# Four array quarters and two PSUM banks for a depthwise convolution, and a last pass with six banks, in a four-layer state-space network

## The chip, the cores and the metric

The kernel runs on one core of a Trainium2 chip. The metric is the device time of one launch in microseconds (us). A core has five engines that each work through their own instructions in order: TensorE (PE in the profile, with its weight loads as PEld), VectorE (DVE), ScalarE (ACT), GpSimd (POOL) and SyncE (SP), which here issues every DMA. Engines wait for one another by semaphores.

## The reference

Four layers run over four images of 64 x 64 pixels with 96 channels. Each layer is a token mixer and a feed-forward block, both with a residual sum and a normalisation ahead. The mixer of layer 0 is a gated linear recurrence over the 4096 pixels. Layers 1 to 3 are selective scans, with 192 inner channels, 16 states and four orders in which the pixels are visited:

```python
xz = ln(x) @ in_proj.T ; u, z = split(xz)        # 192 channels each
u = silu(conv3x3_depthwise(u) + conv_b)          # each channel with its own 9 taps
for each of 4 orders:                            # rows, columns, and both reversed
    delta, B, C = projections(u)
    h[t] = exp(delta[t] * A) * h[t-1] + delta[t] * u[t] * B[t]
    y[t] = C[t] . h[t] + D * u[t]
x = x + (ln(y1 + y2 + y3 + y4) * silu(z)) @ out_proj.T
x = x + feed_forward(ln(x))                      # operands rounded to an 8-bit float
```

The change touches the depthwise convolution of `u`, and the last mixer end and feed-forward block of the last image. What is computed stays the same.

## The kernel before, in words

**Three parts in a row.** `gated` (lines 1050 to 1283) does layer 0 of all images. `scans` (860 to 1047) does twelve stages, one for each pair of layer 1 to 3 and image. Line 1303 then finishes the last image alone: it joins the four orders, normalises, gates, projects out, and runs the feed-forward block.

**A stage of scans.** A stage has 24 items: two directions, four segments of 1024 pixels, three chunks of 128 rows. An item has 16 steps, one for each state, so the twelve stages have 4608 steps. In a step DVE multiplies a row block in PSUM (`bc`) by `du`, and then runs the scan that makes `h`. `bc` comes from PE (`b_rows`, line 904), from two buffers of two banks each; `b_rows(k + 1)` is issued in step `k` and can overwrite its buffer only after the scan of step `k - 1`. ACT makes `da`, POOL multiplies `h` by `c`, and PE adds the products up in `acc` (`add_quarters`, line 940). `add_quarters` uses the array as four tiles of 64 x 64, with 512 columns each, and the two row halves of the array write two different banks.

**What runs beside the steps.** While stage `s` scans, a `Job` (708 to 738) does the rest of the work between the stages for the next one, as Python generators whose `yield`s cut it into rounds. `between` (616 to 706) makes them: first `joins`, `mixers` and `feeds` (the end of the layer before), then `takes` (normalisation and `in_proj`) and `convolves`. Each of these handles 8 strips of 512 pixels. `Job.step` is called once in each step of the scan, and adds `rate` to a credit; each whole credit is one round, in which every chain of the job advances to its next `yield`. So the rate, 1.65 rounds a step, sets where in a stage the job's instructions stand. In the instruction stream of PE they stand after `b_rows(k + 1)` and ahead of `accumulate(k - 3)`. Two other chains advance once a step ahead of the job: `chain` (`prepare_chunk`, the next item's `dt_proj` and `delta`) and `segment` (`next_segment`, the next segment's `x_proj`). At step 0 of each third chunk line 1004 drains `segment` at once, as far as its second `x_proj_b`; at step 13 lines 1022 to 1024 drain both. In stage step 22.4 (item 22, step 4) the job has to be done.

**Banks.** PSUM has eight banks here: four for `bc`, two for `acc`, and two (`tag="ps"`, lines 123 to 132) that all of the above share. `banks["free"]` is a count kept at build time. A chain that has yielded `True` does not advance while no bank is free; one that has yielded a function waits until it returns true. A released bank counts as free from the end of the step (`settle`).

**The convolution.** `convolve` (564 to 614) computes one strip. The first 128 channels are nine matmuls with a diagonal 128 x 128 matrix of taps (`tap_lo`) over 512 pixels, all into one bank, one round each; an ACT copy takes the bank to SBUF. The last 64 channels stand twice on the partitions, and take six matmuls (`tap_hi`).

**Normalisations.** `Norm.measure` puts a variance on the list `pending`. `logarithms` (240) takes the logarithm of all pending ones on ACT, and only then `Norm.settle` can exponentiate and refine on POOL. In `Job.step`, logarithms are taken when no chain could advance for `patience` rounds, and elsewhere by the scan's own code. In line 1303 the patience is 1 and the rate 1.4.

Of the kernel before, what the change touches and what calls it, by code (L numbers as in the profile page):

```python
# [10 lines left out]
F32 = mybir.dt.float32  # L11
# [7 lines left out]
HW = 64  # L19
# [6 lines left out]
T = 1024  # L26
MM = 512
G = MM // 128
NSTRIP = L // MM
SR = MM // HW  # L30
# [69 lines left out]
def metaformer(ctx: ExitStack, tc: tile.TileContext, x, l0_ab, l0_rest, ssm, ffn, out):  # L100
# [8 lines left out]
    pbc = ctx.enter_context(tc.tile_pool(name="pbc", bufs=2, space=bass.MemoryType.PSUM))  # L109

    def sb(bufs, tag, shape, dtype=F32):
        return pools[bufs].tile(shape, dtype, tag=tag, name=tag)

    def const(name, shape, dtype=F32):
        return pools[1].tile(shape, dtype, name=name)

    def wide():
        return pbc.tile([128, T], F32, tag="bc", name="bc")


    banks = {"free": 2, "back": 0}

    def bank(name):
        banks["free"] -= 1
        return pbc.tile([128, MM], F32, tag="ps", name=name)

    def release():
        banks["back"] += 1

    def settle():  # L130
        banks["free"] += banks["back"]
        banks["back"] = 0
# [107 lines left out]
    def logarithms():  # L240
        for n in pending:
            act.activation(n.r, n.v, AF.Ln)
            n.known = True
        pending.clear()
# [319 lines left out]
    def convolve(im, layer, s, hold):  # L564

        lo, hi = hold["pads"].pop(s)
        taps = weights[layer]
        w = taps.w
        raw = []
        groups = (  # L570
            [(taps.lo[:, t, :], lo[:, t // 3 : t // 3 + SR, t % 3 : t % 3 + HW]) for t in range(9)],
            [(taps.hi[:, t, :], hi[:, 0:SR, t : t + HW]) for t in range(3)]
            + [(taps.hi[0:64, 3 + t, :], hi[0:64, 2 : 2 + SR, t : t + HW]) for t in range(3)],
        )
        for i, group in enumerate(groups):
            ps = bank("conv")
            for at, (lhs, rhs) in enumerate(group):
                pe.matmul(ps, lhs, rhs, start=at == 0, stop=at == len(group) - 1)
                yield
            v = sb(1, f"u{i}", [128, MM])  # L580
            act.copy(v, ps)
            release()
            yield i == 0
            raw.append(v)
        for i, v in enumerate(raw):
            act.activation(v, v, AF.Silu, bias=w[:, W_CB + i : W_CB + i + 1])
        gate_z(im, s + 1, hold)
        yield
        yield
        t = slice(s * MM, (s + 1) * MM)  # L590
        cols_a, part_c = hold["cols"]
        sp.dma_start(out=im.u[0, 0:64, t], in_=raw[0][0:64])
        sp.dma_start(out=im.u[1, 0:64, t], in_=raw[0][64:128])
        sp.dma_start(out=im.u[2, 0:64, t], in_=raw[1][0:64])
        for p, src, dst, c0, nc_ in (
            (slice(0, 128), raw[0], cols_a, 0, HW),
            (slice(0, 64), raw[1], part_c, 0, HW // 2),
            (slice(64, 128), raw[1], part_c, HW // 2, HW // 2),
        ):
            pool.tensor_copy(  # L600
                dst[p].rearrange("p (c r) -> p r c", r=HW)[:, SR * s : SR * s + SR, :],
                src[p].rearrange("p (r c) -> p r c", c=HW)[:, :, c0 : c0 + nc_],
            )
            if p.start or p.stop == 128:
                yield
        if s == NSTRIP - 1:
            yield
            sp.dma_start(out=im.u[1, 64:128, :], in_=cols_a[0:64])
            sp.dma_start(out=im.u[0, 64:128, :], in_=cols_a[64:128])
            for k in range(2):  # L610
                sp.dma_start(
                    out=im.u[2, 64:128, k * L // 2 : (k + 1) * L // 2],
                    in_=part_c[64 * k : 64 * k + 64],
                )

    def between(im, layer, dst=None):


        hold = {"in": {}, "pads": {}, "z": {}}
        new = dram.tile([L, C], F32, tag="x", name="x") if dst is None else dst  # L620

        def columns():
            return sb(1, "cols_a", [128, L]), sb(1, "part_c", [128, L // 2])

        def first():
            if layer:
                cols_a, part_c = hold["cols"] = columns()
                sp.dma_start(out=cols_a[0:64], in_=im.y[1, 64:128, :])
                sp.dma_start(out=cols_a[64:128], in_=im.y[0, 64:128, :])
                for k in range(2):  # L630
                    sp.dma_start(
                        out=part_c[64 * k : 64 * k + 64],
                        in_=im.y[2, 64:128, k * L // 2 : (k + 1) * L // 2],
                    )
                load_y(im, 0, hold)
            yield
            yield
            yield

        yield [Chain(first())]  # L640
        done = {"y": 0, "x": 0, "end": 0}

        def joins():
            for s in range(NSTRIP):
                yield lambda: done["x"] > s - 2
                yield True
                yield from join_orders(im, s, hold)
                done["y"] += 1

        def mixers():  # L650
            for s in range(NSTRIP):
                yield lambda: done["end"] > s - 2 and (
                    layer == 0 or (done["y"] > s and hold["y", s][1].known)
                )
                if layer:
                    yield from mixer_out(im, layer, s, hold)
                else:
                    yield from measure_x(im, s, hold)
                done["x"] += 1

        def feeds():
            for s in range(NSTRIP):
                yield lambda: done["x"] > s and hold["x", s][1].known
                yield from feed_forward(im, layer, s, hold, new)
                done["end"] += 1

        yield [Chain(f()) for f in (feeds, mixers, joins)[: 3 if layer else 2]]
        if dst is not None:
            return

        def second():
            if layer + 1 not in weights:
                weights[layer + 1] = Weights(layer + 1)
                for _ in range(4):
                    yield
                weights[layer + 1].derive()
                for t in range(0, 15, 3):
                    yield
                    weights[layer + 1].derive_taps(range(t, t + 3))
            im.x = new  # L680
            im.u = dram.tile([3, 128, L], F32, tag="u", name="u")
            im.z = dram.tile([DI, L], F32, tag="z", name="z")
            hold["cols"] = columns()
            hold["in"][0] = load_x(im, 0)
            yield
            yield

        yield [Chain(second())]
        done = {"in": 0, "out": 0}

        def takes():
            for s in range(NSTRIP):
                yield lambda: done["out"] > s - 3
                yield from take_in(im, layer + 1, s, hold)
                done["in"] += 1

        def convolves():
            yield lambda: done["in"] > 0
            gate_z(im, 0, hold)
            for s in range(NSTRIP):  # L700
                yield lambda: done["in"] > min(s + 1, NSTRIP - 1)
                yield True
                yield from convolve(im, layer + 1, s, hold)
                done["out"] += 1

        yield [Chain(f()) for f in (convolves, takes)]

    class Job:
# [23 lines left out]
                    logarithms()  # L732
                    self.waited = 0

        def finish(self):
            while not self.done:
                self.step()
                settle()


# [545 lines left out]
    for i, im in enumerate(images):  # L1286
        im.src = x[i * L : (i + 1) * L, :]
        im.dst = out[i * L : (i + 1) * L, :]
    with tc.tile_pool(name="pl0", bufs=1, space=bass.MemoryType.PSUM) as pl0:
        gated(images, Job(between(images[0], 0), 2.6, patience=1), pl0)  # L1290
    stages = [(im, layer) for layer in range(1, 4) for im in images]
    jobs = []
    for at in range(len(stages)):
        jobs.append([])
        if at + 1 < len(stages):
            im, layer = stages[at + 1]
            jobs[-1].append(Job(between(im, layer - 1), 1.65))

        for im in {10: images[:2], 11: images[2:3]}.get(at, ()):
            jobs[-1].append(Job(between(im, 3, im.dst), 2.6))  # L1300
    with tc.tile_pool(name="pac", bufs=1, space=bass.MemoryType.PSUM) as pac:
        scans(stages, jobs, pac)
    Job(between(images[-1], 3, images[-1].dst), patience=1).finish()

# [115 lines left out]
```

## Time and profile before

| what | us |
|---|---|
| median of 3 runs (lowest, highest) | 19681.59 (19680.81, 19689.28) |
| the profiled execution, its own time | 19688.32 |
| its span, first to last instruction | 19686.5 |
| layer 0, up to the first scan of 1024 | 1817.2 |
| twelve stages of scans, first to last scan's start | 17574.1 |
| from the last scan's start to the end | 295.2 |

The profile comes from one execution. A group's line gives engine, operation, output and inputs, count, then busy time in us and the mean duration of one in ns, and after the last bar the idle time of the engine just ahead of it with what ended it. All lines stand on L78, because one helper issues every operation, so groups are told apart by their tiles: `bc` and `h` are the two DVE operations of a step, `conv` the convolution, `acc` the sum, `y_t` the joins, `x_proj_b` and `x_proj_c` the segment's projections. An fp32 matmul stands as two records. PEclk is the share of TensorE's full clock that was granted.

### The profile page before, as it was taken

What the parts mean: (1) busy time and instruction counts of PE and PEld (TensorE: products, weight loads), DVE (VectorE), ACT (ScalarE), POOL (GpSimd) and SP (SyncE); (2) the same over time, 40 slices, a digit from 0 to 9 for tenths busy, and PEclk for the clock granted to TensorE, in tenths of its full rate; (3) what the DMA queues carried; (4) which work ended last, traced back from release to release, by engine and by line L of the source; (5) the groups of instructions that cost most, each with busy time, mean ns of one, the idle gap of its engine ahead of it and who ended that gap; (6) DMA issues with size and microseconds to landing.
All of it is one profiled execution on the core that took longest, in us unless ns stands there. A gap on an engine that the chain in (4) does not pass through costs nothing. (4 is left out here: it accounts for less than half of the span.)

```text
span 19686.5 us, 224801 instructions
## 1 busy us (share of the span) xinstructions
PE 16267.7 (83%) x70400; PEld 4750.9 (24%) x70400; DVE 17666.9 (90%) x13768; ACT 12256.8 (62%) x19331; POOL 15495.8 (79%) x10086
## 2 busy tenths in 40 slices
PE   8998787787888887787887888787888888888876
PEld 3332121121122222222222222222222222222223
DVE  6757999999999999999999999999999999998884
ACT  4544665665665665665666666666666666666664
POOL 3435888888888888888888888888888888878884
PEclk9998787787887797797797787797887787787886
DMA  2213676666676667666666676666666666676663
GB/s 52 50 48 87 169 185 168 170 187 164 171 189 173 166 184 182 168 185 178 170 188 176 170 186 172 170 188 174 171 186 172 170 189 174 171 187 169 165 176 89
DMA packets 1269876, 3192.65 MB, mean 162 GB/s; under 512 B 440336, under 2 KB 440560, under 8 KB 1262544
## 3 DMA queue, kind: packets, MB, share of 16 engines
q1 hardware_dynamic: 1268688, 3178.27, 61.5%
q8 instruction: 568, 9.31, 0.2%
q14 instruction: 620, 5.08, 0.1%
HBM read 2818.81 MB, written 308.28 MB: 159 GB/s over the span
## 5 line engine op out<-in xcount | busy, mean ns | idle before, releaser
L78 POOL TENSOR_TENSOR c<-h,c 128x1024 f32<-128x1024 f32 (+1 forms) x4992 | 11334.8, 2277 | 3377.8 <-DVE h L78 1478.0
L78 DVE TENSOR_TENSOR_SCAN h<-da,carry,bc 128x1024 f32<-128x1024 f32 x4608 | 10795.4, 2343 | 530.3 <-POOL c L78 17.0
L78 PE MATMUL acc<-c,twice 64*64 64x512 f32 x36864 | 6215.7, 751 | 20.1 <-POOL c L78 20.0
L78 ACT ACTIVATE da<-delta,decay 128x1024 f32<-128x1024 f32 x4608 | 5280.9, 1147 | 1491.5 <-DVE h L78 1475.6
L78 DVE TENSOR_TENSOR bc<-du,bc 128x1024 f32<-128x1024 f32 x4608 | 5565.6, 1208 | 488.4 <-PE bc L78 461.6
L78 PE MATMUL bc<-bs,sel 96*128 96x512 bf16 x9216 | 3384.4, 455 | 2343.3 <-DVE h L78 2235.9
L78 ACT COPY carry<-h 128x1 f32<-128x1 f32 x3456 | 649.5, 188 | 3374.5 <-DVE h L78 3368.7
L78 PEld LDWEIGHTS <-sel 96*128 96x128 bf16 x9216 | 552.2, 101 | 7301.0 <-DVE h L78 5519.2
L78 PEld LDWEIGHTS acc<-c,twice 64*64 64x64 f32 x36864 | 1130.7, 153 | 2799.4 <-issue 1860.2
L78 ACT ACT_TABLE_LOAD x1155 | 1481.9, 1283 | 36.5 <-DVE mv L78 20.3
L78 PE MATMUL conv<-pad,tap_lo 128*128 128x512 f32 x1728 | 906.5, 634 | 0.0
L78 PE MATMUL dt_proj<-rows,w 12*128 12x512 f32 x1152 | 826.5, 804 | 6.4 <-ACT delta L78 6.4
L78 ACT ACTIVATE du<-e,ones 128x1024 f32<-128x1024 f32 x576 | 659.3, 1145 | 199.3 <-POOL delta L78 194.5
L78 POOL TENSOR_TENSOR delta<-delta,du 128x1024 f32<-128x1024 f32 x288 | 679.8, 2361 | 72.0 <-ACT du L78 70.3
L78 PE MATMUL x_proj_b<-u,xp 128*108 128x512 f32 x1152 | 687.6, 713 | 46.4 <-DMA xp<-in_ssm 15.5
L78 PE MATMUL x_proj_c<-u,xp 128*32 128x512 f32 x1152 | 642.0, 672 | 76.1 <-ACT rows L78 67.0
L78 POOL TENSOR_TENSOR e<-e,du 128x1024 f32<-128x1024 f32 x288 | 679.8, 2360 | 2.4 <-ACT du L78 2.4
L78 ACT ACTIVATE c<-c,l_bias 128x512 f32<-128x512 f32 x384 | 263.6, 686 | 670.5 <-PE c L78 665.9
L78 POOL TENSOR_TENSOR du<-delta,u 128x1024 f32<-128x1024 f32 x288 | 680.4, 2363 | 0.1
L78 POOL TENSOR_TENSOR delta<-delta,e 128x1024 f32<-128x1024 f32 x288 | 678.8, 2357 | 0.1
L78 PE MATMUL conv<-pad,tap_hi 128*128 128x512 f32 (+1 forms) x1152 | 601.8, 624 | 0.6 <-ACT u L78 0.5
L78 DVE TENSOR_TENSOR_SCAN h<-da,l_carry,bc 128x512 f32<-128x512 f32 x384 | 491.4, 1280 | 41.9 <-DVE bc L78 2.3
(152 smaller groups left out, 15200.8 us busy)
## 6 DMA issues: line engine op xcount, KB each, us to landing
c<-cs SPq DMA_DIRECT2D x9216, 256.0 KB, 4.2
u<-u SPq DMA_DIRECT2D x288, 512.0 KB, 6.7
y<-y SPq DMA_DIRECT2D x1152, 128.0 KB, 3.2
y<-y SPq DMA_DIRECT2D x144, 512.0 KB, 6.8
xr<-x SPq DMA_DIRECT2D x224, 192.0 KB, 5.1
u<-u SPq DMA_DIRECT2D x288, 128.0 KB, 3.6
pad<-y SPq DMA_DIRECT2D x288, 128.0 KB, 4.9
z<-zl SPq DMA_DIRECT2D x96, 256.0 KB, 2.0
```

What stands on the lines that cost most here:

```text
L78: ins = f(*a, **k).ins
```

## The change

- Nine matmuls of 128 x 128 by 512 columns become nine times four of 64 x 64 by 256 columns: only the diagonal quarters of the taps, for each half of the channels and each half of the strip's eight rows. The two halves of the channels write two banks.
- One ACT copy of 128 x 512 becomes four of 64 x 256.
- `convolves` starts a strip only when both shared banks are free. The second part takes a bank after that, as before.
- `bc` moves to a PSUM pool of its own, closed after the last stage; a pool of six banks then serves the last image.
- The rate of the job between stages rises from 1.65 to 1.75.
- The last image runs at a rate of 3, with six banks, and takes logarithms after each step in which any are pending.

```diff
+        raw = [sb(1, f"u{i}", [128, MM]) for i in range(2)]
+        two = [bank("conv_a"), bank("conv_b")]
+        half = SR // 2
+        for t in range(9):
+            for k in range(2):
+                p = slice(64 * k, 64 * k + 64)
+                for j in range(2):
+                    o, y = 64 * (j ^ k), t // 3 + half * j
+                    pe.matmul(
+                        two[k][o : o + 64, 0 : MM // 2],
+                        taps.lo[p, t, p],
+                        lo[p, y : y + half, t % 3 : t % 3 + HW],
+                        start=t == 0,
+                        stop=t == 8,
+                        tile_position=(64 * k, o),
+                    )
+            yield
+        for k in range(2):
+            p = slice(64 * k, 64 * k + 64)
+            for j in range(2):
+                o = 64 * (j ^ k)
+                act.copy(raw[0][p, j * MM // 2 : (j + 1) * MM // 2], two[k][o : o + 64, 0 : MM // 2])
             release()
...
-                yield True
+                yield lambda: banks["free"] > 1
                 yield from convolve(im, layer + 1, s, hold)
...
-        def finish(self):
+        def finish(self, eager=False):
             while not self.done:
                 self.step()
+                if eager and pending:
+                    logarithms()
                 settle()
...
-            jobs[-1].append(Job(between(im, layer - 1), 1.65))
+                jobs[-1].append(Job(between(im, layer - 1), 1.75))
...
-    Job(between(images[-1], 3, images[-1].dst), patience=1).finish()
+    with tc.tile_pool(name="pend", bufs=6, space=bass.MemoryType.PSUM) as pend:
+        banks.update(free=6, back=0, pool=pend)
+        Job(between(images[-1], 3, images[-1].dst), 3, patience=1).finish(eager=True)
```

More of the change, by code (lines that the diff above doesn't have):

```diff
@@ L115, in const @@
         return pools[1].tile(shape, dtype, name=name)
+    wides = []
     def wide():
-        return pbc.tile([128, T], F32, tag="bc", name="bc")
-    banks = {"free": 2, "back": 0}
+        return wides[0].tile([128, T], F32, tag="bc", name="bc")
+    banks = {"free": 2, "back": 0, "pool": pbc}
     def bank(name):
         banks["free"] -= 1
-        return pbc.tile([128, MM], F32, tag="ps", name=name)
+        return banks["pool"].tile([128, MM], F32, tag="ps", name=name)
     def release():
@@ L568, in convolve @@
         w = taps.w
[L569 to L581, printed above, removed]
-            release()
-            yield i == 0
-            raw.append(v)
+        raw = [sb(1, f"u{i}", [128, MM]) for i in range(2)]
[20 more added lines that the diff above has]
+                act.copy(raw[0][p, j * MM // 2 : (j + 1) * MM // 2], two[k][o : o + 64, 0 : MM // 2])
+            release()
+        yield True
+        ps = bank("conv")
+        group = [(taps.hi[:, t, :], hi[:, 0:SR, t : t + HW]) for t in range(3)]
+        group += [(taps.hi[0:64, 3 + t, :], hi[0:64, 2 : 2 + SR, t : t + HW]) for t in range(3)]
+        for at, (lhs, rhs) in enumerate(group):
+            pe.matmul(ps, lhs, rhs, start=at == 0, stop=at == len(group) - 1)
+            yield
+        act.copy(raw[1], ps)
+        release()
+        yield
         for i, v in enumerate(raw):
@@ L1288, in metaformer @@
         im.dst = out[i * L : (i + 1) * L, :]
[L1289 to L1296, printed above, removed]
-            jobs[-1].append(Job(between(im, layer - 1), 1.65))
[L1299 to L1302, printed above, removed]
-    Job(between(images[-1], 3, images[-1].dst), patience=1).finish()
+    with tc.tile_pool(name="pbig", bufs=2, space=bass.MemoryType.PSUM) as wides_pool:
+        wides.append(wides_pool)
+        with tc.tile_pool(name="pl0", bufs=1, space=bass.MemoryType.PSUM) as pl0:
+            gated(images, Job(between(images[0], 0), 2.6, patience=1), pl0)
+        stages = [(im, layer) for layer in range(1, 4) for im in images]
+        jobs = []
+        for at in range(len(stages)):
+            jobs.append([])
+            if at + 1 < len(stages):
+                im, layer = stages[at + 1]
+                jobs[-1].append(Job(between(im, layer - 1), 1.75))
+            for im in {10: images[:2], 11: images[2:3]}.get(at, ()):
+                jobs[-1].append(Job(between(im, 3, im.dst), 2.6))
+        with tc.tile_pool(name="pac", bufs=1, space=bass.MemoryType.PSUM) as pac:
+            scans(stages, jobs, pac)
+    with tc.tile_pool(name="pend", bufs=6, space=bass.MemoryType.PSUM) as pend:
+        banks.update(free=6, back=0, pool=pend)
+        Job(between(images[-1], 3, images[-1].dst), 3, patience=1).finish(eager=True)
 def _layer0(W_in, b_in, W_out, b_out, gamma, beta):
```

## The prediction, made before the changed kernel was run

> **What bounds the kernel now.** I read the page first, then DVE's waits, then busy time by stretch, and last the timeline around single waits.
>
> ```profile
> PEclk9998787787887797797797787797887787787886
> L78 DVE TENSOR_TENSOR_SCAN h<-da,carry,bc 128x1024 f32<-128x1024 f32 x4608 | 10795.4, 2343 | 530.3 <-POOL c L78 17.0
> L78 PE MATMUL acc<-c,twice 64*64 64x512 f32 x36864 | 6215.7, 751 | 20.1 <-POOL c L78 20.0
> L78 DVE TENSOR_TENSOR bc<-du,bc 128x1024 f32<-128x1024 f32 x4608 | 5565.6, 1208 | 488.4 <-PE bc L78 461.6
> L78 PE MATMUL conv<-pad,tap_lo 128*128 128x512 f32 x1728 | 906.5, 634 | 0.0
> ```
>
> The twelve stages belong to DVE: 1.208 + 2.343 = 3.551 us a step, and successive steps start 3.604 us apart where nothing disturbs them. 4608 x 3.604 = 16607 of the 17574 us. Of the other 967, DVE's own smaller work (joins, normalisations, `x_proj` remainders) is some 750. So faster matmuls can only win where PE makes DVE wait. The view of DVE's waits, over the scans:
>
> ```profile
> DVE bc L78 <- PE bc L78: 461.6, 271, 20.7
> DVE x L78 <- PE out_proj L78: 29.9, 24, 3.4
> ```
>
> 461.6 us is all there is, with 21 us of it one wait. Where it lies decides. Busy time by stretch: layer 0 while it convolves, the last image's fill and run, a convolving part of stage 4 (items 13 to 20), and the part ahead of it:
>
> ```profile
> core 0: us, PE busy (x) PEld busy (x) DVE busy (x) ACT busy (x) POOL busy (x), PEclk, DMA share, GB/s
> 940.00:1480.00 540.00, 498.82 (x1249) 196.17 (x1249) 292.50 (x384) 242.66 (x494) 181.61 (x330) 0.93 0.19 47
> ...
> 19391.00:19421.00 30.00, 3.19 (x21) 0.45 (x17) 2.56 (x2) 1.01 (x1) 3.91 (x2) 0.59 0.68 147
> 19421.00:19687.00 266.00, 174.75 (x856) 108.91 (x856) 30.22 (x144) 103.02 (x226) 64.86 (x136) 0.50 0.13 33
> 8355.00:8845.00 490.00, 435.32 (x1808) 119.94 (x1804) 459.66 (x270) 343.58 (x553) 415.99 (x256) 0.92 0.69 184
> 7568.00:8355.00 787.00, 628.02 (x3168) 196.43 (x3168) 744.03 (x627) 515.07 (x811) 668.17 (x411) 0.80 0.67 173
> ```
>
> Three different limits. Layer 0 is PE's (92% busy, DVE 54%). In the stages DVE is at 94%. The end is nobody's: PE 66%, ACT 39%, all waiting in chains. DVE's waits (us in total, times, longest) in the convolving part of stage 4:
>
> ```profile
> DVE bc L78 <- PE bc L78: 9.8, 5, 4.0
> ```
>
> and in the part ahead of it, where no convolution runs:
>
> ```profile
> DVE bc L78 <- PE bc L78: 21.9, 15, 5.0
> ```
>
> **Two rules of the Trainium skill.** "TensorEngine Tiling (Array Packing)", Theoretical Speedup, offers up to four times for operands small in both dimensions; Key Properties adds that a change of tiling mode drains the array. The trace has the same four-quarter form in `acc`: 6215.7 us / 36864 records x 8 = 1.349 us for four quarters of 512 columns, against 2 x 0.525 = 1.049 us (906.5 / 1728) for a full matmul of 512. So quarters run together, at 1.29 times the price. I go by this row: half the columns, about 0.67 us a tap.
>
> "TensorE: Matmul & The Clock Gate", What's actually happening, says that too little activity drops the array to half rate. Here the granted clock is 0.92 where the convolution runs, 0.80 ahead of it, and 0.50 all through the end although PE is 66% busy there. Taking work off PE may therefore lower its clock, and in the stages I do not turn saved PE time into time one for one; for the end I go by 0.50 again.
>
> **The change part by part.** Sums are against the profiled execution, 19688.3 us (span 19686.5, 1.8 around it); the median 19681.6 lies 6.7 lower, and the forecast takes the same difference from it.
>
> *1. The taps in layer 0.* Eight strips have 72 taps. In the layer-0 stretches the tiles of `conv` hold PE for 123.97 us in 240 records, 1.033 us a tap. Against 0.67: 0.36 x 72 = 26 us. If the extra 0.30 us of a quarter group is fixed (0.52 + 0.30 = 0.82), 15; with no overhead (0.52), 37. Both banks held at once can delay the next strip's preparation; counting rounds, it ends at step 7 to 9 of 12 instead of 7, in time for the next strip. With PE 92% busy I take **-20** (range -37 to +10).
>
> *2. The taps in the stages.* 88 strips. PE loses 88 x 9 x (1.05 - 0.67) = 300 us of work, but DVE waits only 9.8 us a stage there. One of the five waits (4.0 us) falls in a stretch of `dt_proj`, `x_proj_c` and `acc` with no convolution in it; another (3.3) partly waits for `in_xt` on ACT. I give the taps 4 us a stage: 11 x 4 = **-44** (range 0 to -108).
>
> *3. The four copies.* ACT rows: 0.582 us for 128 x 512, 0.252 for 128 x 64, hence an estimated 0.39 for 256 columns. Four are 1.57 instead of 0.58: +1 us a strip, 96 us in all on an engine that is 70% busy there. `da`, queued behind them, is issued two steps ahead, and DVE waits 7 us for it in all. **0**; uncovered, at most 1 us a strip.
>
> *4. Both banks.* I counted the order round by round, for both versions, as the code writes it. For the version before, the count puts the convolutions in items 13 to 20, as the trace does. For the new one, with 1.75, the job still ends by step 21.7, ahead of its limit at 22.4, so no stage stops for it. While the taps hold both banks (nine rounds), `chain`, `segment` and `takes` cannot take one. `segment` then runs late, and line 1004 must draw 2 to 4 of its rounds at once, ahead of `b_rows(k + 1)`: about three times a stage, never before the change. Such a draw holds three `x_proj` matmuls, 3 x 1.19 (2 x 0.596) = 3.6 us of PE. `b_rows` runs a step ahead, which covers about as much at full clock and less at a low one. I take 1 us each: 11 x 3 = **+33** (range 0 to 4 us each, +132).
>
> *5. The rate.* The joins' first matmul moves from step 4 of a stage to step 3. It waits for a DMA:
>
> ```profile
> 7589.28 0.77 PE L78 MATMUL y_t<-ident,pad 128*128 128x128 f32 x2 [5.69 <-DMA pad<-y]
> ...
> 7594.65 1.23 DVE L78 TENSOR_TENSOR bc<-du,bc 128x1024 f32<-128x1024 f32 x1 [4.96 <-PE bc L78]
> ```
>
> Behind it on PE stand `acc` and the next `b_rows`, for which DVE waits. The landing stays, the matmul stands one step earlier, so DVE stops up to 3.6 us longer, in the eight stages whose job begins with joins: 0 to +29; I take 2.5 each, **+20**. SP's loads stand where they stood, at step 0. The rest of the joins gets 6% denser and the item after the job emptier: 0.
>
> *6. The end.* Its first 30 us (last sum, store, loads) stay. Then 266 us hold 174.75 us of PE work. Before, logarithms wait until every chain stands still:
>
> ```profile
> POOL t L78 <- ACT norm L78: 127.2, 6, 49.1
> DVE st L78 <- ACT yt L78: 100.5, 16, 32.7
> ```
>
> and of ACT's groups there:
>
> ```profile
> L78 ACT ACT_TABLE_LOAD x10 | 12.8, 1283 | 0.1
> ```
>
> Ten table loads are five groups of logarithms, as the count has it; then come 16 single ones, so up to 32 loads, +28 us on ACT, which has 103 of 266 in use. In return the three chains no longer stop together, and with six banks none waits for one. From 19421 to 19600 PE was busy 136.6 of 179 us (76%); fully interleaved work reaches 92% in layer 0. At 85%: 174.75 / 0.85 = 206, plus the last strip's way through the feed-forward block, some 18 us (19653 to 19671 in the chain), is 224 instead of 266: **-42**. Ends: all of PE's time back to back, 175 + 18, -73; the added loads on the chain and nothing won, +28.
>
> Sum: -20 - 44 + 0 + 33 + 20 - 42 = **-53**: 19635 in that execution, **19629** as a median (-0.27%).
>
> **Rivals.**
> - *The end doesn't shrink* (its chain is latency, and table loads eat what eager logarithms win): -20 - 44 + 53 = -11, **19671**. For it: ACT, POOL and DVE each wait over 60 us there for one another. Against: PE idles 24% even where three strips could overlap.
> - *Slower: the draws at the third chunks.* Place: PE ahead of `b_rows` at step 0 of an item. At 4 us each (the size of the largest such wait in the part above) 132, with the joins at 29: -20 - 44 - 42 + 161 = +55, **19737**. The draws decide against the change from 86 / 33 = 2.6 us each on. For it: PE is 89% busy there and cold at times; against: a step of slack.
> - *The convolution frees all of its part:* 11 x 9.8 = -108, layer 0 -37, end -73, joins +20, draws 0: -198, **19484**. Against it: the 4 us wait without a convolution.
> - *The quarters don't run together*, four times 0.52 = 2.1 us a tap: the `acc` row excludes it.
>
> **How the numbers follow.** A measurement of this kernel tells about 0.2% (39 us) from no change. Forecast 0.54, with its own range 19600 to 19665, of which 0.46 lies below 19642; end flat 0.20; slower 0.14; all freed 0.12. Faster 0.46 + 0.12 = 0.58, same 0.08 + 0.20 = 0.28, slower 0.14. The range goes from 19550 to 19720: it leaves out about half of each outer rival.
>
> **What would show it.** `conv<-pad,tap_lo` with four times the records and 0.52 to 0.82 us of PE per tap; the 461.6 us between 430 and 480; first waits of a stage near 7.5 us; new waits of DVE at step 0 or 1 of items 14, 17 and 20; the end at 240 to 265 us from the last scan's start, at clock 0.50, with about 30 table loads. I am wrong if the wait for PE drops by 150 us, if the draws cost over 2.6 us each, or if the clock in the end rises.

## The result, and the profile after

The change makes the kernel slower: 19813.76 us (median of 4 runs, 19794.9 to 19825.05) against 19685.43 (4 runs, 19680.81 to 19696.65), a ratio of 1.0066 with a 95% interval from 1.0054 to 1.0078. The forecast was 19629. The profiled execution took 19825.05 us, its span is 19823.2. Cut at the same three points as before:

| part | before | after | difference | forecast |
|---|---|---|---|---|
| layer 0 | 1817.2 | 1754.4 | -62.8 | -20 |
| twelve stages of scans | 17574.2 | 17849.8 | +275.6 | +9 |
| from the last scan's start | 295.2 | 219.1 | -76.1 | -42 |

Both outer parts won more than forecast, and the stages lost it all. The page of after, with the lines that answer to those shown of before:

```profile
PEclk9998786786887897887887887797887887888786
L78 DVE TENSOR_TENSOR_SCAN h<-da,carry,bc 128x1024 f32<-128x1024 f32 x4608 | 10797.5, 2343 | 559.7 <-ACT da L78 34.3
L78 PE MATMUL acc<-c,twice 64*64 64x512 f32 x36864 | 6163.7, 745 | 39.7 <-POOL c L78 39.7
L78 DVE TENSOR_TENSOR bc<-du,bc 128x1024 f32<-128x1024 f32 x4608 | 5571.4, 1209 | 677.1 <-PE bc L78 651.0
```

DVE's two operations of a step last as long as before, to the nanosecond or one off. What grew stands behind the last bar: the wait for PE ahead of `bc` went from 461.6 to 651.0 us. The groups of PE, the taps now in two tiles:

```profile
L78 PE MATMUL conv_a<-pad,tap_lo 64*64 64x256 f32 x3456 | 502.2, 403 | 0.0
L78 PE MATMUL conv_b<-pad,tap_lo 64*64 64x256 f32 x3456 | 501.6, 403 | 5.6 <-ACT zh L78 5.6
```

The two tiles run side by side. Together they hold PE for 514.4 us (the records' union), 0.595 us for each of 864 taps, against 906.5 us and 1.049 before. So the change does to PE what it says. Busy time by stretch: layer 0 while it convolves, the last image's fill and run, the convolving part of stage 4, and the part ahead of it:

```profile
910.00:1440.00 530.00, 497.12 (x1758) 195.70 (x1756) 316.31 (x415) 257.26 (x547) 191.82 (x349) 0.94 0.20 49
19604.00:19640.00 36.00, 9.37 (x59) 4.76 (x56) 3.01 (x4) 1.49 (x2) 3.74 (x2) 0.58 0.77 166
19640.00:19824.00 184.00, 156.25 (x818) 105.17 (x818) 29.13 (x142) 112.17 (x233) 65.00 (x136) 0.50 0.15 40
8310.00:8840.00 530.00, 419.88 (x2240) 117.22 (x2240) 474.19 (x276) 348.46 (x567) 425.52 (x273) 0.88 0.65 174
```

In the end PE is 85% busy instead of 66%, still at clock 0.50. In the convolving part of stage 4 PE fell from 89% to 79%, its clock from 0.92 to 0.88, and DVE's share from 94% to 89%: PE has less to do, and DVE waits for it more. DVE's waits there were 9.8 us for `bc` and 2.2 for `rows`; now:

```profile
DVE bc L78 <- PE bc L78: 26.6, 15, 4.9
DVE rows L78 <- ACT bs L78: 10.0, 3, 4.3
DVE h L78 <- ACT da L78: 4.2, 4, 2.5
```

What PE itself waits for tells why. Before, over the whole run (us in total, times, longest):

```profile
PE y_t L78 <- DMA pad<-y: 116.5, 12, 23.3
PE in_xt L78 <- ACT xh L78: 64.4, 41, 5.8
PE z L78 <- ACT pad L78: 1.3, 3, 0.4
PE in_proj L78 <- ACT hq L78: 0.4, 1, 0.4
```

And after:

```profile
PE y_t L78 <- DMA pad<-y: 160.6, 12, 23.2
PE z L78 <- ACT pad L78: 97.7, 37, 7.2
PE in_proj L78 <- ACT hq L78: 58.8, 15, 5.8
PE in_xt L78 <- ACT xh L78: 17.8, 13, 4.4
```

`in_proj` and `z` belong to `takes`, and both waits are new: 1.7 us became 156.5. One of them in the timeline of stage 4 (start and duration in us, the idle time ahead of it in brackets):

```profile
8514.48 0.38 PE L78 MATMUL conv_a<-pad,tap_lo 64*64 64x256 f32 x2
...
8522.99 1.06 PE L78 MATMUL in_xt<-ident,xh 128*96 128x128 f32 x4
...
8527.56 1.12 PE L78 MATMUL dt_proj<-rows,w 12*128 12x512 f32 x2
...
8541.90 1.02 PE L78 MATMUL in_proj<-hq,w 96*128 96x512 f32 x2
...
8548.61 1.28 ACT L78 ACT_TABLE_LOAD   x1
8549.91 1.15 ACT L78 ACTIVATE du<-e,ones 128x1024 f32<-128x1024 f32 x1
...
8551.14 1.28 ACT L78 ACT_TABLE_LOAD   x1
8552.43 1.15 ACT L78 ACTIVATE da<-delta,decay 128x1024 f32<-128x1024 f32 x1
...
8553.49 1.37 ACT L78 COPY pad<-in_proj 64x512 f32<-64x512 f32 x3
...
8554.91 1.97 PE L78 MATMUL z<-hq,w 96*64 96x512 f32 x2 [7.22 <-ACT pad L78]
...
8558.73 1.04 PE L78 MATMUL bc<-bs,sel 96*128 96x512 bf16 x2
...
8559.80 1.23 DVE L78 TENSOR_TENSOR bc<-du,bc 128x1024 f32<-128x1024 f32 x1 [3.79 <-PE bc L78]
```

Read from the top: the taps end at 8514.9 and give their banks back. Then `takes` (`in_xt`) and `prepare_chunk` (`dt_proj`), which both had waited for a bank, run side by side, and what they ask of ACT queues there one behind the other. `prepare_chunk`'s `du<-e` and the table loads stand ahead of the copy that empties `in_proj`'s bank. `z` stops PE for 7.22 us until that copy is done, `bc` stands behind `z` in PE's stream, and DVE loses 3.79 us. In the step before, DVE had lost 2.46 us to `da`, which stood behind the same `du<-e` and table loads.

### The profile page after: what moved, and what is told of

It reads as the page before. It is cut to its first block, busy times and chain, and to the rows that moved or that the text cites. A ratio compares the mean times of both kernels' runs of the same rounds, so it can differ in the third digit from the quotient of the medians.

```text
span 19823.2 us, 235330 instructions
## 1 busy us (share of the span) xinstructions
PE 15940.5 (80%) x75584; PEld 4692.2 (24%) x75584; DVE 17681.6 (89%) x13768; ACT 12257.0 (62%) x19560; POOL 15494.2 (78%) x10086
## 5 line engine op out<-in xcount | busy, mean ns | idle before, releaser
L78 DVE TENSOR_TENSOR bc<-du,bc 128x1024 f32<-128x1024 f32 x4608 | 5571.4, 1209 | 677.1 <-PE bc L78 651.0
L78 PEld LDWEIGHTS acc<-c,twice 64*64 64x64 f32 x36864 | 1178.9, 153 | 2601.7 <-issue 1709.7
L78 PE MATMUL conv<-pad,tap_hi 128*128 128x512 f32 (+1 forms) x1152 | 675.8, 693 | 0.2 <-ACT u L78 0.2
L78 PE MATMUL y_t<-ident,pad 128*128 128x128 f32 (+1 forms) x1536 | 413.8, 359 | 162.6 <-DMA pad<-y 160.6
```

The costliest lines, as they stand in the source:

```text
L78: ins = f(*a, **k).ins
```

## The experiments

Fifteen kernels, each with a profile and timed beside the kernel before. The table splits the profiled executions as above; the last column compares medians with the kernel before on the same chip and in the same session, where its median was 19667.8 to 19685.4.

| kernel | layer 0 | stages | end | median | ratio (95%) |
|---|---|---|---|---|---|
| before | 1817.2 | 17574.2 | 295.2 | 19685.43 | |
| after | 1754.4 | 17849.8 | 219.1 | 19813.76 | 1.0066 (1.0054 to 1.0078) |
| a1_end_only | 1805.7 | 17583.4 | 218.7 | 19609.55 | 0.9965 (0.9953 to 0.9978) |
| a2_order_only | 1772.3 | 17799.5 | 295.1 | 19862.91 | 1.0094 (1.0080 to 1.0108) |
| a3_taps_only | 1797.5 | 17594.1 | 294.7 | 19679.56 | 0.9997 (0.9989 to 1.0006) |
| a4_rate_only | 1806.2 | 17557.4 | 295.2 | 19647.58 | 0.9987 (0.9981 to 0.9994) |
| b4_end_two_banks | 1800.2 | 17581.4 | 235.8 | 19619.49 | 0.9971 (0.9960 to 0.9982) |
| c1_order_half_taps | 1760.1 | 17813.0 | 295.5 | 19856.88 | 1.0092 (1.0078 to 1.0106) |
| c2_rate_two | 1776.4 | 17810.4 | 218.0 | 19802.28 | 1.0062 (1.0049 to 1.0075) |
| c3_start_only | 1786.9 | 17594.3 | 295.3 | 19692.94 | 1.0011 (1.0005 to 1.0018) |
| c4_best | 1761.7 | 17554.6 | 218.5 | 19545.78 | 0.9932 (0.9920 to 0.9944) |
| d1_takes_wait | 1761.4 | 17591.2 | 295.5 | 19630.92 | 0.9977 (0.9969 to 0.9984) |
| d2_scan_chains_wait | 1793.1 | 17680.4 | 295.1 | 19771.51 | 1.0047 (1.0033 to 1.0060) |
| d3_four_copies | 1766.1 | 17832.7 | 295.2 | 19879.00 | 1.0102 (1.0088 to 1.0115) |
| e1_segment_free | 1773.5 | 17601.7 | 295.4 | 19680.84 | 1.0003 (0.9995 to 1.0011) |
| e2_chunk_free | 1769.4 | 17697.2 | 295.3 | 19775.26 | 1.0058 (1.0045 to 1.0071) |
| e3_takes_spread | 1766.7 | 17744.2 | 217.5 | 19730.53 | 1.0035 (1.0022 to 1.0049) |

How far a single execution carries: layer 0 has the same code in before, a1, a4 and b4, and took 1800 to 1817 us; the stages have the same code in before, a1 and b4, and took 17574 to 17583. But 33 executions of the kernel before, timed beside the first kernels, lie between 19641 and 19703 us. So a difference of less than some 40 us between two single executions is not read unless the medians bear it out.

### The four parts, each alone

**a1_end_only** takes the changed last line and what it needs, with the old convolution and rate:

```diff
-    Job(between(images[-1], 3, images[-1].dst), patience=1).finish()
+    with tc.tile_pool(name="pend", bufs=6, space=bass.MemoryType.PSUM) as pend:
+        banks.update(free=6, back=0, pool=pend)
+        Job(between(images[-1], 3, images[-1].dst), 3, patience=1).finish(eager=True)
```

> The kernel before, with the change's last part alone: bc in a PSUM pool of its own, six banks, a rate of 3 and early logarithms for the last image. If the three parts of the kernel add up: layer 0 and the stages stay within 10 us, the stretch after the last scan's start falls from 295 to about 219 us, the whole is some 76 us faster (about 19610). If the new pool of bc disturbs the stages: they lengthen by tens of us.

Measured: the end is 218.7 us, a gain of 76.5, and the whole kernel 0.9965. The end's part is real and stands by itself.

**a2_order_only** keeps the nine full matmuls, and holds the second bank in the count only, so that every chain moves as in the changed kernel:

```diff
             ps = bank("conv")
+            if i == 0:
+                idle = bank("idle")
...
             release()
+            if i == 0:
+                release()
...
-                yield True
+                yield lambda: banks["free"] > 1
...
-            jobs[-1].append(Job(between(im, layer - 1), 1.65))
+            jobs[-1].append(Job(between(im, layer - 1), 1.75))
```

> The order of the changed kernel without its cheaper taps: full 128 x 128 taps into one bank as before, but a strip starts only with both banks free and holds both while its taps run, at a rate of 1.75; end as before. If holding both banks is the cause of the loss: the stages lengthen by 276 us or more (up to 400, as the taps stay long). If the quarters or their four copies are the cause: the stages lengthen by less than 60 us.

Measured: the stages take 17799.5 us, +225 of the +276 without one quarter matmul. That is short of the 276 that were expected, but far above 60. Most of the loss is the order, not the form of the taps. The same order gives layer 0 a gain of 45.

**a3_taps_only** keeps the order and the rate of before, and computes half the taps' columns (256 of 512 pixels of the first 128 channels; the others are left out):

```diff
-                pe.matmul(ps, lhs, rhs, start=at == 0, stop=at == len(group) - 1)
+                if i == 0:
+                    pe.matmul(ps[:, 0 : MM // 2], lhs, rhs[:, 0 : SR // 2], start=at == 0, stop=at == 8)
```

> The order before, rate 1.65, one bank, with half of the taps' columns left out (256 of 512 pixels of the first 128 channels are computed, and copied twice): PE's time for a tap as short as that of four quarters. If PE's time for the taps was worth anything in the stages: they shorten by 40 to 110 us. If the stages do not wait for the taps: by less than 20. Layer 0 shortens by 25 to 60 us.

Measured: 0.9997, no difference. The stages took 17594.1 us, not less. Layer 0, at 1797.5, is 3 to 20 us below the kernels with the same code there, where 25 to 60 had been expected. Busy time over exactly the stages, the kernel before:

```profile
1817.20:19391.30 17574.10, 14492.50 (x65358) 4018.93 (x65358) 16463.35 (x11918) 11330.46 (x17389) 14732.42 (x8757) 0.81 0.67 176
```

and a3_taps_only:

```profile
1797.50:19391.60 17594.10, 14225.20 (x65358) 4044.59 (x65358) 16461.10 (x11918) 11335.99 (x17477) 14723.52 (x8757) 0.80 0.67 175
```

PE has 267 us less to do, DVE has the same work, and the span is no shorter. In the stages the saved time is off the path.

**a4_rate_only** changes 1.65 to 1.75 and nothing else.

> The kernel before with a rate of 1.75 in place of 1.65, nothing else. If both banks are the cause: the stages lengthen by 20 to 60 us (the joins' first matmul waits a step longer for its DMA in eight stages, and a denser job). If the rate is the cause: by 150 to 276 us.

Measured: the stages are 17 us shorter and the whole 0.9987. The view of PE's waits has the joins' wait that the prediction spoke of, 116.5 us before:

```profile
PE y_t L78 <- DMA pad<-y: 152.5, 11, 22.9
```

DVE's waits behind it rose from 90 to 120 us, and the rest of the denser job gave back more than that.

**b4_end_two_banks** has the end's rate of 3 and its early logarithms, but the two banks of before.

> The end with its rate of 3 and early logarithms, but two banks as before instead of six. If the early logarithms carry the end's gain: from the last scan's start 219 to 240 us. If the banks carry it: 265 to 295. Layer 0 and the stages as before.

Measured: 235.8 us. Of the end's 76, rate and logarithms give 59, the four further banks 17.

### Which part of the order costs

**c1_order_half_taps** is a2 with a3's half columns (same 256 pixels left out). **d3_four_copies** is c1 with four copies of 64 x 256 instead of two of 128 x 256:

```diff
-                for j in range(2):
-                    act.copy(v[:, j * MM // 2 : (j + 1) * MM // 2], ps[:, 0 : MM // 2])
+                for k in range(2):
+                    p = slice(64 * k, 64 * k + 64)
+                    for j in range(2):
+                        act.copy(v[p, j * MM // 2 : (j + 1) * MM // 2], ps[p, 0 : MM // 2])
```

> The order-only kernel with half of the taps' columns left out (256 of 512 pixels, copied twice): the changed kernel's order and its PE time for a tap, but whole-array matmuls and two copies instead of quarters and four. Order-only took 17799 us in the stages, the changed kernel 17850. If the quarters and their four copies cost the 50 us between them: about 17790 here. If a shorter tap itself is worth nothing or worse in this order (a lower clock, another alignment): 17830 to 17860.

> The order-only kernel with half of the taps' columns left out, and four copies of 64 x 256 as in the changed kernel instead of two (stages 17813 us with two, changed kernel 17850). If the copies carry the difference: 17840 to 17860. If the quarter matmuls carry it: 17800 to 17825.

Measured: stages 17813.0 and 17832.7, against 17799.5 with full taps. Halving the taps wins nothing in the new order either. The copies may cost 20 us, and the quarters against half matmuls 17 more (17849.8); neither is clear of the scatter. Both results lie between the ranges that were set for the two readings, so they decide for neither.

**c3_start_only** makes a strip wait until both banks are free, but gives the second back in the same step:

```diff
+            if i == 0:
+                idle = bank("idle")
+                release()
```

> The order-only kernel, but the second bank is given back in the round in which it is taken: a strip still starts only when both are free, rate 1.75. If holding the bank through nine rounds is the cause: the stages stay within 40 us of the rate-only kernel (17557). If waiting for both to be free is: they lengthen to 17700 or more.

Measured: stages 17594.3, +37 against a4 and far from a2's 17799.5. The medians bear the +37 out, as the two intervals in the table do not meet; 28 us of it are a longer wait of DVE for `da`. So it is the holding through nine rounds that costs most, and the next four kernels hold only some chains. All have the both-banks start and the rate of 1.75, and refuse a bank by the chain's kind while the taps run; **d1_takes_wait** refuses `takes`, **d2_scan_chains_wait** both scan chains:

```diff
-        elif chain.need and banks["free"] < 1:
+        elif chain.need and (banks["free"] < 1 or (held["now"] and chain.kind == "takes")):
             return False
```

> Full taps into one bank at a rate of 1.75, a strip starting with both banks free, as in the order-only kernel (stages 17800 us); but while the taps run only takes may not use the other bank, and chain and segment may. If the loss comes from takes being pushed behind the taps: the stages stay at 17720 or more, with z waiting for ACT. If it comes from chain and segment (draws): 17560 to 17640, and rows wait for ACT about 30 us.

> The mirror image: while the taps run chain and segment may not use the other bank, and takes may. If the loss comes from chain and segment: the stages stay at 17720 or more, rows wait for ACT 80 us or more, z hardly waits for ACT. If it comes from takes: 17560 to 17640.

**e1_segment_free** refuses `takes` and `chain` (`prepare_chunk`), **e2_chunk_free** `takes` and `segment`:

> As the runs that hold one kind of chain while the full taps run (one bank, rate 1.75, start with both free), but takes and the chunk's chain are held and segment is free. If the loss needs segment: 17590 to 17630 in the stages and rows waiting about 30 us. If the pair takes and chunk makes it: 17680 or more, with z waiting for ACT 60 us or more.

> Takes and segment are held while the full taps run, the chunk's chain is free. If the pair takes and segment makes the loss: 17720 to 17800 in the stages, rows waiting 80 us or more. If the chunk's chain is needed: 17600 to 17680.

Measured, all inside the scans and in us: the stages against c3's 17594.3, three waits of DVE, and what PE waits for ACT ahead of `z` and `in_proj`:

| held through the taps | stages | DVE: `bc` for PE | `rows` for ACT | `da` for ACT | PE: `z` + `in_proj` | longest `z` |
|---|---|---|---|---|---|---|
| none (c3) | 0 | 500 | 25 | 32 | 27 | 3.2 |
| takes (d1) | -3 | 541 | 3 | 6 | 110 | 2.8 |
| takes, chunk (e1) | +7 | 536 | 25 | 7 | 83 | 3.0 |
| chunk, segment (d2) | +86 | 500 | 120 | 22 | 1 | none |
| takes, segment (e2) | +103 | 538 | 104 | 18 | 116 | 3.0 |
| all three (a2) | +205 | 599 | 107 | 26 | 137 | 7.2 |

Each kernel's median, less layer 0 and end from its profile, gives -37, +1, +73, +100 and +185 instead, so the stages' column is good to some 40 us. d1 and e1 came out where `segment` was to carry the loss; d2 and e2 fell between the ranges set for their two readings.

Two costs come out. Where `segment` is held, `rows` waits 104 to 120 us instead of 25, and 86 to 103 us are lost: the draws. With about 33 draws that is 2.6 to 3.1 us each. One of them in the timeline of the changed kernel, at step 0 of item 14 in stage 4:

```profile
8461.22 2.83 PE L78 MATMUL x_proj_b<-u,xp 128*108 128x512 f32 x6
...
8466.67 0.69 DVE L78 TENSOR_TENSOR rows<-x_proj_b,bs 96x512 f32<-96x512 f32 x1 [3.79 <-ACT bs L78]
```

DVE does not stop for `b_rows` here, but for the operation that ends the draw's own chain: PE's six `x_proj_b` records, ACT's cast to `bs`, then `rows` on DVE. By place, thirty of the waits for `rows` in d2 and in e2, with 91 and 93 us, stand at step 0 of items 14, 17 and 20; in c3 it is twelve with 18.

The second cost, another 100 us, is there only when all three chains are held. The lines of d1, which loses nothing:

```profile
DVE bc L78 <- PE bc L78: 540.5, 300, 22.7
PE z L78 <- ACT pad L78: 72.2, 39, 2.8
```

and of a2:

```profile
DVE bc L78 <- PE bc L78: 599.4, 321, 22.9
PE z L78 <- ACT pad L78: 91.9, 33, 7.2
```

Waiting for `z` and `in_proj` is therefore no loss by itself: in d1 it comes with 41 us more for `bc`, and 48 less for `rows` and `da`. Against e2, the nearest kernel, a2's DVE waits 95 us longer in all, 61 of them for `bc`, and single waits for `z` reach 7.2 us, as in the timeline of the result. e1, which holds and lets go `takes` and `prepare_chunk` alone, loses nothing, so their meeting on ACT is not enough without `segment` held too; why, no run shows. `segment` held alone was not run.

**e3_takes_spread** attacks the second cost in the changed kernel: one more round after `in_xt` and after each `in_proj` before the next matmul of `takes` may be issued, with the rate at 1.85 to make up for it.

```diff
         release()
+        yield
...
             release()
+            yield
...
-                jobs[-1].append(Job(between(im, layer - 1), 1.75))
+                jobs[-1].append(Job(between(im, layer - 1), 1.85))
```

> The changed kernel with one more round after each of takes' in_xt and in_proj, and a rate of 1.85 so that the job still ends in time. If takes' way through one bank (z and in_proj waiting for ACT) carries the part that only all three make: those waits fall from some 100 us to under 30, and the stages shorten by 70 to 130 us from 17850. If it is the mere crowding after the taps: the waits fall, but the stages stay within 40 us.

Its waits of PE:

```profile
PE z L78 <- ACT pad L78: 29.6, 23, 2.0
PE in_proj L78 <- ACT hq L78: 1.7, 1, 1.7
```

and of DVE:

```profile
DVE bc L78 <- PE bc L78: 529.8, 302, 25.6
DVE rows L78 <- ACT bs L78: 67.9, 27, 14.7
```

156.5 us of waits for `z` and `in_proj` became 31.3, and the stages 106 us shorter than in the changed kernel. As `rows` fell too (113.8 to 67.9), part of the 106 is draws, and a higher rate alone gave 39 us in c2 below. So the run supports `takes`' part in the second cost and doesn't size it.

**c2_rate_two** is the changed kernel at a rate of 2.0, which gets the job through a stage earlier and so moves the convolutions to other items.

> The changed kernel with a rate of 2.0 instead of 1.75. Counting rounds, the draws of segment at the third chunks fall from 12 rounds in a stage to 2. If the draws carry most of the loss: the wait of DVE's rows for ACT falls from 96 us to about 35 and the stages shorten by 100 us or more. If takes, squeezed through one bank, carries it: rows falls all the same, but the stages stay above 17750, with z and in_proj still waiting for ACT.

Measured: `rows` fell from 96 to 26 us inside the scans, but the stages only from 17849.8 to 17810.4. The denser job brings waits of its own: DVE for `xh` from POOL 12 to 59 us, for `out_proj` 18 to 44. A rate does not cure it.

### A version that keeps what won

**c4_best** uses quarters and both banks only for the one convolution beside layer 0, the old convolution in the stages, with the rate of 1.75 and the changed end:

```diff
+    def early(im, layer):
+        return layer == 1 and im is images[0]
...
-                yield lambda: banks["free"] > 1
+                yield (lambda: banks["free"] > 1) if early(im, layer + 1) else True
```

> Quarters and both banks only for the first image's strips, which run beside layer 0; the stages as before with a rate of 1.75; the changed end. If the parts add up: layer 0 near 1755 us, the stages near 17557, the end near 219, in all about 19535 to 19560, faster than both kernels.

Measured: 19545.78 us, 0.9932 (0.9920 to 0.9944), faster than both kernels. Layer 0 gives 56, the stages 20, the end 77. Its page has the wait for PE nearly where it was before:

```profile
L78 DVE TENSOR_TENSOR bc<-du,bc 128x1024 f32<-128x1024 f32 x4608 | 5566.3, 1208 | 513.7 <-PE bc L78 486.6
```

## Why the prediction was wrong, step by step

**1. The taps in layer 0 (-20, measured -63).** The execution before has the longest layer 0 of the four with the same code, so the gain is 46 to 63. The sign was right, and most of the gain is not the taps', so the sign was in part luck. The half taps alone (a3) give 1797.5 against 1800 to 1817 with untouched code. What was missed is a wait of PE beside the third image of layer 0, before:

```profile
PE in_xt L78 <- ACT xh L78: 22.7, 7, 5.8
```

It is 0.4 us at most in all kernels in which `takes` can get no bank in the step in which a strip starts (3.3 in e3): `in_xt` is issued later, when ACT has `xh` ready. d2, in which `takes` is not held, has the both-banks start and still 22.0 us of it, and layer 0 took 1793.1. c3, which keeps the second bank for one step, has 0.4 and took 1786.9; with `takes` held through the taps (d1) it is 1761.4, the granted clock from 840 us to 40 us before the end of layer 0 is 0.96 instead of 0.92, and the records of `tap_lo` take 599 ns instead of 636. Why the clock is higher there was not settled.

**2. The taps in the stages (-44, measured nothing).** PE's saving was sized well enough: 300 us forecast, 262 measured (14492.5 to 14230.7 busy in the stages). Its worth was not. I had read 9.8 us a stage as waits in the convolving part and gave the taps four. Take DVE's waits for `bc` of at least 0.3 us inside the scans, 455 us in all, one by one, and ask what PE did in the 3.6 us ahead: under 20 us have PE at work without a wait and the convolution in it. The others have joins, `out_proj` or `x_proj_c` there, or PE standing idle for another engine. That trace was at hand. So was a sum that did not close: of the 967 us outside undisturbed steps I gave 750 to DVE's smaller work, and 217 cannot hold 461.6 us of waits. The 750 are durations of records, many of which overlap the scans'.

The Trainium skill ("TensorE: Matmul & The Clock Gate", What's actually happening) has the array's rate follow its activity. The traces agree in part: from the first to the last record of `conv` in each of eleven stages the mean clock was 0.93 with PE 90% busy (before) and 0.91 with the taps halved and PE 85% busy (a3). But e2 had 0.93 at 86% and d2 0.91 at 89%, and in the end the clock stayed at 0.50 while PE went from 66% to 85% busy.

**3. The four copies (0).** Some 20 us, not clear of the scatter and inside the bound of 96 that was kept.

**4. Both banks (+33, measured some 240): the step that failed.** It counted which chains would be late and priced one consequence, the draws, at 1 us each. Their place was right: 25 of DVE's waits for `rows`, with 78 us, now stand at step 0 of items 14, 17 and 20. Their price was not. They cost 2.6 to 3.1 us each, past the 2.6 that I had named as a sign of being wrong, since their chain runs through ACT and ends on DVE, where a step of slack on `b_rows` doesn't help. `takes` and `prepare_chunk` were counted as late and put at nothing. That left out 37 us for the start with both banks free, and another 100 that come when all three chains are held. Chains held together are let go together: in the timeline of the result, `prepare_chunk` and `takes` share ACT's queue, and `takes`' next matmul stands in PE's stream ahead of `bc` before ACT has emptied the bank.

From before to after DVE's waits inside the scans rise by 189 us for `bc`, 68 for `rows` and 27 for `da`. Sorted as in step 2, the waits for `bc` with PE idle for `z` ahead of them are 74 us and those with `in_proj` 30, both none before; those behind the joins' wait rise by 35, and those with the convolution and no wait of PE from 18 to 95. This says where the waits stand and not what causes the loss. The last class is 55 us already with the rate alone (a4), which is no loss, and the first two make 71 in d1, which loses nothing against c3.

From kernel to kernel, each time between single executions, the stages run 17574 - 17 (rate) + 37 (start) + 205 (held) + 14 (half taps) + 20 (copies) + 17 (quarters) = 17850. Of these only 37 and 205, and the 17 of the rate, are clear of the scatter by the medians.

**5. The rate (+20).** The joins' wait came as argued: +30 us, 2.7 each over 11 stages where I had 2.5 over eight. "The rest 0" was wrong: a denser job won 47 back.

**6. The end (-42, measured -76).** The clock stayed at 0.50, and PE reached the 85% assumed. Two terms were mis-sized. The same 876 records of PE from the last scan's start cover 166 us instead of 178, which at 85% is 14 us. Their durations sum to 357 us and 360, so they are hardly shorter; they overlap more. And the last strip's way of 18 us is not on top of the 85%, it lies inside: 36 us of fill and 184 of run make 220, where the forecast had 30 + 206 + 18. The logarithms cost less than feared:

```profile
L78 ACT ACT_TABLE_LOAD x18 | 23.1, 1283 | 0.3
```

18 table loads instead of 10, not some 30, and +10 us on ACT. POOL's wait for them fell from 127.2 us in six waits to 53.2.

The quarters themselves were forecast at 0.67 us a tap (0.52 to 0.82), measured 0.595. The page "TensorEngine Tiling (Array Packing)", The Solution, counts four independent tiles of 64 x 64. The trace comes near that: a full matmul with 256 columns takes 0.549 us in c1, which has the same order, so four in a row would take an estimated 2.20 us, and the four quarters together take 0.595. Against the full matmul with twice the columns they are 1.76 times as fast. The drain between tiling modes that the prediction cites is not seen by itself in any run.

The slower rival had the right place for about a third of the loss, but another wait: DVE stops for `rows`, not for `b_rows`. Its price of 4 us a draw, 132 in all, is above the 86 to 103 found, and its 19737 lies 77 below the result, because what comes when all three chains are held was not in it.

**Open:** why the second 100 us need `segment` held beside `takes` and `prepare_chunk`, and how they split between `z`, `in_proj` and later `da`; whether `segment` alone costs as much as with another chain; and the clock in layer 0.

## What to carry to other kernels

Price work taken off an engine by the waits that stand directly behind that work: 267 us off TensorE in the stages were worth nothing measurable (a3), as under 20 us of waits stood behind it. When a scarce buffer is held longer, list every chain that must wait for it, what all of them issue on being let go together, and who stands behind that in each in-order queue. To tell an order from a cost, build the kernel that has the new order with the old operations, and the one that has the old order with cheaper operations; here the first gave +225 us in the stages and the second no difference.

## What the hardware showed that I had not expected

- In the last image TensorE kept a granted clock of 0.50 at 85% busy, with small, mostly fp32 matmuls and 105 us of weight loads in 184 us.
- Busy time of TensorE is not a fixed amount of work to be divided by a share: the same 876 matmul records from the last scan's start covered 178 us before and 166 after, though their durations sum to 360 and 357. With fewer pauses between them they overlap more.
